# A four-layer stack on one core: which of every four scan steps hands its last product to GpSimd

## The chip, the cores and the metric

The kernel runs on one core of one Trainium2 chip. A core has five engines with a queue of instructions each: TensorE (PE, matmuls and transposes), VectorE (DVE), ScalarE (ACT), GpSimd (POOL) and SyncE (SP), which issues most of the transfers. An engine takes its instructions in order and waits at one whose operands are not ready. The metric is the time of one execution on the device in microseconds; the median over several runs counts.

## The reference, cut to what matters

Four layers follow each other over x of 4 x 512 x 256: a cross-attention block (L0), a self- and cross-attention block (L1), four selective-scan (Mamba) blocks (L2) and another attention block (L3). The change lies in L2. Each of its four blocks computes for every batch and each of 512 channels e, with 16 states s:

```
dt  = softplus(dt_low @ dtp_w + dtp_b)
dA  = exp(dt[..., None] * A)                        # decay of a state
dBu = dt[..., None] * Bm[:, :, None, :] * xi[..., None]
h   = da * h + dbu                                  # over time t
y_t = sum over s of h[e, s] * c[s]                  # the output map C
y   = (y + xi * D) * silu(z)
```

xi is a convolution of the block's input with a silu; Bm, Cm and dt_low are projections of xi.

## The kernel before, in words

Channels lie on the 128 partitions in four chunks (EC = 4), time on the free axis (T = 512). A **unit** is one block and one batch; there are 16 (NU), in order of block, then batch. A unit has two **pairs** of channel chunks, and a pair takes 16 **steps**: each step handles one chunk and two states, so one instruction covers 128 x 1024 values. Steps alternate between the two chunks of the pair; two steps share the loaded rows of B and C for their two states. A unit has 32 steps, all units together 512. In the text r is the step's number within its unit, from 0 to 31.

What a step i does:

- `maps` (L1625): SP loads the rows of B and C, spread over the partitions, as bB (3 buffers) and bC (4 buffers), four and five steps ahead.
- `product` (L1632): POOL computes dBu = dtx * bB, two steps ahead; dBu has four buffers. `begin` (L1649): ACT writes the start values into its first columns.
- `decay` (L1644): ACT computes two exponentials into ps_dA, a PSUM tile with two buffers, one step ahead.
- `states` (L1659): DVE runs the scan over time. 
- Then the states are multiplied by bC. For three steps of four DVE does it: the scan has written back into ps_dA, and `outputs_here` (L1666) multiplies ps_dA by bC into hC, four buffers. For the fourth, which `on_gpsimd` names, the scan writes to hP in SBUF (two buffers), and `outputs` (L1670) lets POOL multiply hP by bC in place, one step later.
- `add_up` (L1692): PE transposes and sums the products into ps_y: eight instructions of a 128 x 128 tile. DVE's products are added two steps after their scan, POOL's three steps after.

After 16 steps `close_pair` (L1708) lets DVE multiply ps_y by the gate zs into g, at the second step of the next pair. Beside the steps generators run that work out the next unit's input, advanced twice in each step: `front` (norm L1379 to L1421, ps_in by L185, xp L1443, convolution ps_cv by L178, xi L1430, xd L1468), `step` (ps_dt L1498, dt L1500, softplus L1309, dtx L1511, start values L1513 to L1519), `gate` (ps_z by L185, zs L1541), `gated` (ps_gt L1559, gT L1562, ps_out, hT_res L1574). The silus of xi and zs (`flush_silu`, L1723) come at r = 10 and 15. With the first batch of a block `front` also makes the block's diagonal weights on POOL (w_dg L1394, w_dD L1400).

The order on each queue is written out by hand, as one loop over the steps. Each pass issues, in this order: the silus, the loads, the exponentials of the next step, POOL's product two steps ahead, POOL's output of the step before, the closing of a pair, the scan, the transposes, and DVE's output, with the generators between.

Of the kernel before, what the change touches and what calls it, by code (L numbers as in the profile page):

```python
# [117 lines left out]

def on_gpsimd(i):

    return i % 4 == 1


@with_exitstack
def kernel(ctx: ExitStack, tc: tile.TileContext, t: dict, out: bass.AP):
# [1185 lines left out]
    def layer2(hT, A, far, h63, tail, X, fw, wl, late):  # L1311
# [5 lines left out]
        with ExitStack() as st:  # L1317
# [333 lines left out]
            def states(i):  # L1651
                if on_gpsimd(i):
                    hC = pool.tile([P, 2, T], F32, name="hP", tag="hP", bufs=2)
                else:
                    hC = pool.tile([P, 2, T], F32, name="hC", tag="hC", bufs=4)
                hCs[i] = hC
                dA = dAs[i].rearrange("p s t -> p (s t)")
                to = hC.rearrange("p s t -> p (s t)") if on_gpsimd(i) else dA
                nc.vector.tensor_tensor_scan(  # L1659
                    to, dA, dBus.pop(i).rearrange("p s t -> p (s t)"), 0.0, ALU.mult, ALU.add  # L1660
                )

            def outputs_here(i):
                dA = dAs.pop(i)
                if not on_gpsimd(i):
                    nc.vector.tensor_mul(hCs[i], dA, bmap[i // 2, 1])  # L1666
# [388 lines left out]
```

## Time and profile before

| | us |
|---|---|
| median of three runs | 4141.29 |
| lowest and highest | 4137.86, 4146.58 |
| profiled execution | 4144.32 |
| its span | 4142.5 |

| stretch of the span | us | PE busy | DVE busy | ACT busy | POOL busy |
|---|---|---|---|---|---|
| layers 0 and 1, to 1560 | 1560 | 1384 | 908 | 629 | 648 |
| before the first scan, to 1608 | 48 | 32 | 0.5 | 18 | 7 |
| scan block, unit 0, to 1720 | 112 | 94 | 93 | 73 | 97 |
| scan block, units 1 to 15, to 3430 | 1710 | 1373 | 1599 | 1106 | 1544 |
| layer 3 | 712.5 | 632 | 433 | 322 | 93 |

In the page, a group's line gives the line of code, engine, operation, output and inputs, the count, the busy time and the mean of one, and then the idle time of the engine just ahead of it with what ended that. In a timeline a row gives start, duration, engine, line and operands, and in brackets the idle time ahead of it and its releaser. A releaser is inferred: of several things waited for it is the one that came last by the profile.

### The profile page before, as it was taken

What the parts mean: (1) busy time and instruction counts of PE and PEld (TensorE: products, weight loads), DVE (VectorE), ACT (ScalarE), POOL (GpSimd) and SP (SyncE); (2) the same over time, 40 slices, a digit from 0 to 9 for tenths busy, and PEclk for the clock granted to TensorE, in tenths of its full rate; (3) what the DMA queues carried; (4) which work ended last, traced back from release to release, by engine and by line L of the source; (5) the groups of instructions that cost most, each with busy time, mean ns of one, the idle gap of its engine ahead of it and who ended that gap; (6) DMA issues with size and microseconds to landing.
All of it is one profiled execution on the core that took longest, in us unless ns stands there. A gap on an engine that the chain in (4) does not pass through costs nothing. (4 is left out here: it accounts for less than half of the span.)

```text
span 4142.5 us, 48645 instructions
## 1 busy us (share of the span) xinstructions
PE 3515.9 (85%) x17616; PEld 2204.8 (53%) x17616; DVE 3033.5 (73%) x2903; ACT 2148.3 (52%) x4366; POOL 2388.4 (58%) x1625
## 2 busy tenths in 40 slices
PE   7989998988898897888888788888887667999889
PEld 4654554545566464555555555555554444555446
DVE  5547567476555633999999999998999996676653
ACT  2345454454212424666666666666666553556422
POOL 2349269076100425899999999999998881000131
PEclk8999999999998998988988898888888778999999
DMA  2023022033100203444444444444443441000000
GB/s 75 11 85 103 25 82 92 17 96 94 44 1 0 66 22 104 152 150 154 153 159 148 150 157 159 158 153 149 158 154 138 143 155 36 1 1 1 1 6 16
DMA packets 140287, 369.93 MB, mean 89 GB/s; under 512 B 20624, under 2 KB 38224, under 8 KB 140048
## 3 DMA queue, kind: packets, MB, share of 16 engines
q1 hardware_dynamic: 136688, 363.58, 26.1%
q10 hardware_dynamic: 3360, 3.25, 0.3%
q8 instruction: 139, 2.28, 0.2%
q14 instruction: 100, 0.82, 0.1%
HBM read 363.50 MB, written 3.28 MB: 89 GB/s over the span
## 5 line engine op out<-in xcount | busy, mean ns | idle before, releaser
L1632 POOL TENSOR_TENSOR dBu<-dtx,bB 128x1022 f32<-128x1022 f32 x512 | 1199.0, 2362 | 65.9 <-DVE ps_dA L1659 65.9
L1659 DVE TENSOR_TENSOR_SCAN ps_dA<-ps_dA,dBu 128x1024 f32<-128x1024 f32 x384 | 878.3, 2287 | 131.6 <-POOL dBu L1632 91.8
L1644 ACT ACTIVATE ps_dA<-dt,A 128x512 f32<-128x512 f32 x1024 | 708.3, 692 | 428.5 <-DVE hC L1666 365.6
L1692 PE MATMUL ps_y<-ident,hC 128*128 128x128 f32 x3072 | 460.7, 302 | 104.1 <-DVE hC L1666 104.0
L1692 PEld LDWEIGHTS ps_y<-ident,hC 128*128 128x128 f32 x3072 | 403.9, 158 | 193.3 <-DVE hC L1666 122.4
L1666 DVE TENSOR_TENSOR hC<-ps_dA,bC 128x1024 f32<-128x1024 f32 x384 | 470.1, 1224 | 25.5 <-issue 0.4
L967 ACT ACTIVATE pr<-ps_s,nm 128x512 f32<-128x512 f32 x512 | 345.2, 686 | 260.2 <-DVE nm L963 260.2
L963 DVE TENSOR_REDUCE nm<-ps_s 128x2 f32<-128x1024 f32 x256 | 301.4, 1218 | 158.5 <-PE ps_s L952 144.2
L1670 POOL TENSOR_TENSOR hP<-hP,bC 128x1024 f32<-128x1024 f32 x128 | 302.1, 2360 | 89.2 <-issue 38.9
L981 PE MATMUL ps_pt<-ident,pr 128*128 128x128 f32 x2048 | 284.9, 279 | 66.9 <-DVE pT L986 33.2
L981 PEld LDWEIGHTS ps_pt<-ident,pr 128*128 128x128 f32 x2048 | 232.2, 142 | 165.0 <-issue 61.7
L1659 DVE TENSOR_TENSOR_SCAN hP<-ps_dA,dBu 128x1024 f32<-128x1024 f32 x128 | 291.8, 2280 | 2.9 <-ACT dBu L1649 2.2
L616 POOL TENSOR_TENSOR ln_rstd<-ln_rstd,const 128x4 f32<-128x4 f32 x24 | 24.4, 1018 | 443.8 <-DVE ln_rstd L615 442.2
L178 PE MATMUL ps_cv<-xp,w_dg 128*128 128x512 f32 x512 | 248.9, 619 | 30.9 <-ACT dBu L1649 25.3
L535 DVE TENSOR_TENSOR_SCAN phb<-pdA,phb 128x512 f32<-128x512 f32 x128 | 223.8, 1763 | 60.3 <-POOL phb L525 43.8
L984 ACT COPY pT<-ps_pt 128x512 f32<-128x512 f32 x256 | 140.6, 592 | 171.5 <-PE ps_pt L981 170.9
L1000 PE MATMUL ps_o<-pT,V 128*64 128x256 f32 (+1 forms) x2048 | 221.8, 393 | 1.8 <-ACT AT L1018 1.8
L952 PE MATMUL ps_s<-kT,qT 64*128 64x512 f32 (+1 forms) x1024 | 208.3, 644 | 2.2 <-DVE kT L1172 1.4
L525 POOL TENSOR_TENSOR phb<-hT_res,pm 128x512 f32<-128x512 f32 x128 | 188.4, 1476 | 34.0 <-DMA pm<-scrp 20.9
L1692 PE MATMUL ps_y<-ident,hP 128*128 128x128 f32 x1024 | 154.1, 300 | 54.6 <-POOL hP L1670 54.6
L784 POOL TENSOR_TENSOR pr<-pr,rs 128x512 f32<-128x512 f32 x64 | 65.4, 1043 | 225.2 <-DVE rs L782 219.3
L1692 PEld LDWEIGHTS ps_y<-ident,hP 128*128 128x128 f32 x1024 | 132.2, 155 | 109.6 <-POOL hP L1670 63.1
(276 smaller groups left out, 6399.2 us busy)
## 6 DMA issues: line engine op xcount, KB each, us to landing
bB<-scr SPq DMA_DIRECT2D x256, 512.0 KB, 4.1
bC<-scr SPq DMA_DIRECT2D x256, 512.0 KB, 3.8
pm<-scrp SPq DMA_DIRECT2D x224, 256.0 KB, 3.1
w_pw_in<-in_L_in SPq DMA_DIRECT2D x7, 512.0 KB, 4.5
X<-in_x SPq DMA_DIRECT2D x4, 512.0 KB, 7.2
w_L_W<-in_L_W SPq DMA_DIRECT2D x2, 1024.0 KB, 10.4
w_L_Wq<-in_L_Wq SPq DMA_DIRECT2D x2, 1024.0 KB, 6.4
w_L_Wo<-in_L_Wo SPq DMA_DIRECT2D x2, 1024.0 KB, 9.0
```

Source lines behind the costliest of these rows:

```text
L178: nc.tensor.matmul(dst, l, r, start=(i == 0), stop=(i == len(pairs) - 1))
L535: nc.vector.tensor_tensor_scan(hb, dA, hb, 0.0, ALU.mult, ALU.add)
L963: nc.vector.tensor_reduce(nm, ps, AX.X, ALU.max, negate=True)
L967: nc.scalar.activation(pr, ps[:, x, :], AF.Exp, bias=nm[:, x : x + 1], accum_out=rs[:, y : y + 1])
L981: nc.tensor.transpose(pp[:, t4, :], pr[:, t4 * P : (t4 + 1) * P], ident)
L1000: nc.tensor.matmul(ps_o[0][j * stride : (j + 1) * stride, half * W2 : (half + 1) * W2], Vs[n][0][:, t4, h * stride : (h + 1) * stride], pT ...
L1632: nc.gpsimd.tensor_mul(dBu[:, :, 1:], dtx[:, 1:].unsqueeze(1).broadcast_to([P, 2, T - 1]), bmap[i // 2, 0][:, :, 1:])
L1644: nc.scalar.activation(dA, dt, AF.Exp, scale=A[:, l, m, s : s + 1])
L1659: nc.vector.tensor_tensor_scan(to, dA, dBus.pop(i).rearrange("p s t -> p (s t)"), 0.0, ALU.mult, ALU.add)
L1666: nc.vector.tensor_mul(hCs[i], dA, bmap[i // 2, 1])
L1670: nc.gpsimd.tensor_mul(hCs[i], hCs[i], bmap[i // 2, 1])
L1692: nc.tensor.matmul(y[:, j, k * P : (k + 1) * P], hC[:, s, j * P : (j + 1) * P], ident, is_transpose=True, start=False, stop=(2 * s2 + s == ...
```

## The change

POOL multiplies the first step of every four (r = 0, 4, 8, ...) instead of the second (r = 1, 5, 9, ...). The number of products on each engine stays the same. With it move: the scans that write hP, the places of POOL's and DVE's products in their queues, and the transposes of both in PE's queue, since POOL's step is added three steps after its scan and DVE's two.

```
 def on_gpsimd(i):
-    return i % 4 == 1
+    return i % 4 == 0
```

What reads it:

```
def states(i):
    if on_gpsimd(i):
        hC = pool.tile([P, 2, T], F32, name="hP", tag="hP", bufs=2)
    else:
        hC = pool.tile([P, 2, T], F32, name="hC", tag="hC", bufs=4)
...
for j in (i - 3, i - 2):
    if 0 <= j < NU * US and on_gpsimd(j) == (j == i - 3):
        add_up(j)
```

## The prediction

> **What bounds the kernel now.** The views were read from the whole to one step. First the page's busy shares and its 40 slices: they say which engine is full where. In the scan block (1608 to 3430 us; slices 16 to 33) VectorE (DVE) stands at 9 tenths nearly throughout, TensorE and GpSimd (POOL) at 8 to 9.
>
> ```profile
> span 4142.5 us, 48645 instructions
> PE 3515.9 (85%) x17616; PEld 2204.8 (53%) x17616; DVE 3033.5 (73%) x2903; ACT 2148.3 (52%) x4366; POOL 2388.4 (58%) x1625
> DVE  5547567476555633999999999998999996676653
> POOL 2349269076100425899999999999998881000131
> L1659 DVE TENSOR_TENSOR_SCAN ps_dA<-ps_dA,dBu 128x1024 f32<-128x1024 f32 x384 | 878.3, 2287 | 131.6 <-POOL dBu L1632 91.8
> L1666 DVE TENSOR_TENSOR hC<-ps_dA,bC 128x1024 f32<-128x1024 f32 x384 | 470.1, 1224 | 25.5 <-issue 0.4
> L1670 POOL TENSOR_TENSOR hP<-hP,bC 128x1024 f32<-128x1024 f32 x128 | 302.1, 2360 | 89.2 <-issue 38.9
> ```
>
> The change adds and removes no instruction: 384 products stay on DVE, 128 on POOL. So only DVE's idle time between steps can move. I went through DVE's timeline, numbered the scans (512 steps, 16 units of 32, r is the step within its unit) and listed every wait over 0.3 us. They recur at fixed places: before r=11 in all 16 units (4.39 us in unit 0, 3.16 in units 1 to 14, 1.74 in unit 15), before r=3 (2.24 in unit 0, 0.56 in twelve others), before r=19 (0.90 to 1.27 in units 1 to 14), and 4.10 before g in units 3, 7 and 11. The page blames POOL for most of them, so I looked at one, in ScalarE's (ACT) timeline and then DVE's (unit 11, r=8 to 11):
>
> ```profile
> 2888.36 1.42 ACT L1644 ACTIVATE ps_dA<-dt,A 128x512 f32<-128x512 f32 x2 [0.94 <-DVE hC L1666]
> 2889.71 0.18 ACT L1649 COPY dBu<-h 128x2 f32<-128x2 f32 x1
> 2889.89 1.28 ACT L1723 ACT_TABLE_LOAD   x1
> 2891.19 1.92 ACT L1723 ACTIVATE xi<-xi 128x2048 f32<-128x2048 f32 x1
> 2893.01 1.89 ACT L1723 ACTIVATE zs<-zs 128x2048 f32<-128x2048 f32 x1
> 2894.92 1.28 ACT L1644 ACT_TABLE_LOAD   x1
> 2896.21 1.42 ACT L1644 ACTIVATE ps_dA<-dt,A 128x512 f32<-128x512 f32 x2
> ...
> 2884.78 2.29 DVE L1659 TENSOR_TENSOR_SCAN ps_dA<-ps_dA,dBu 128x1024 f32<-128x1024 f32 x1
> 2887.10 1.22 DVE L1666 TENSOR_TENSOR hC<-ps_dA,bC 128x1024 f32<-128x1024 f32 x1
> 2888.24 2.28 DVE L1659 TENSOR_TENSOR_SCAN hP<-ps_dA,dBu 128x1024 f32<-128x1024 f32 x1
> 2890.44 0.67 DVE L1574 TENSOR_TENSOR hT_res<-ps_out,hT_res 128x512 f32<-128x512 f32 x1
> 2891.02 2.29 DVE L1659 TENSOR_TENSOR_SCAN ps_dA<-ps_dA,dBu 128x1024 f32<-128x1024 f32 x1
> 2893.34 1.22 DVE L1666 TENSOR_TENSOR hC<-ps_dA,bC 128x1024 f32<-128x1024 f32 x1
> 2897.73 2.30 DVE L1659 TENSOR_TENSOR_SCAN ps_dA<-ps_dA,dBu 128x1024 f32<-128x1024 f32 x1 [3.17 <-POOL dBu L1632]
> ```
>
> The last exponential of step 11 ends at 2896.21 + 1.42 = 2897.63, the scan starts at 2897.73. The dBu it reads had been made about 9.9 us before (POOL's products counted the same way); POOL merely ended a later one at that moment. So ACT ends this wait: two silus and two table loads stand between the exponentials of steps 10 and 11. At r=3 and r=19 it is the softplus with its two loads.
>
> **The rule that follows.** ps_dA has two buffers, so the exponentials of step r can start when step r-2 has let its buffer go: after its scan if POOL multiplies, after its product if DVE does. From there DVE runs steps r-1 and r before it wants step r+1. A step with its product takes 2.32 + 1.14 = 3.46 us from start to start (2891.02 to 2893.34, 2887.10 to 2888.24), one without 2.20 (2888.24 to 2890.44). Work behind the exponentials of step r therefore has 6.92 us of cover if DVE multiplies both r-1 and r, and 5.66 if POOL takes one of them: 1.26 less. POOL's step is now 1 modulo 4, so the short covers are at r = 1 and 2 modulo 4. After the change they are at 0 and 1: r = 2, 6, 10, 18 gain 1.26, r = 0, 8, 24 lose 1.26, the others keep theirs. The instruction order of the built programs agrees: ACT's and SP's queues are unchanged line for line, only PE, DVE and POOL move.
>
> **Part by part.**
> - r=11, silus behind step 10: 16 waits of at least 1.74, each shorter by 1.26: **-20.2**. At least 0.9 each if ACT isn't free when scan 8 ends.
> - r=3, softplus behind step 2: twelve waits of 0.56 go (-6.7), unit 0's loses 1.26: **-8.0**.
> - r=19, softplus behind step 18: eleven waits (units 1, 3 to 5, 7 to 9, 11 to 14), 10.2 in all, go: **-10.2**. In units 2, 6 and 10 nothing: POOL has four w_dg products and w_dD there, and its next hP product now comes ahead of rstd instead of behind it (2.36 later, less the 1.15 that POOL idled ahead of this burst), so rstd, ps_rb and DVE's hn come 1.2 later, which takes the 0.90.
> - r=25, xi waiting for ps_cv behind step 24: the cover shrinks. The slack between the last exponential and the scan is now 0.1 in units 0, 1 and 11, 0.8 to 1.0 in 5, 8, 9 and 12, about 2 or more elsewhere; 0.1 is the hand-over. Loss: 3 x 1.26 + (0.56 + 0.36 + 0.36 + 0.46) = **+5.5**.
> - r=9, zs waiting for ps_z behind step 8: slack 0.9 in all units, so 0.46 x 16 = 7.4 would be lost. But on PE the fourth ps_z group now stands ahead of step 4's eight transposes instead of behind them, and one group is 0.87 from start to start: taken at **0**, upper end +7.4.
> - r=1, 5, 13, 17, 21, 29: slack 1.2 to 2.6 (most 1.9 or 2.0) against 1.26: 0.
> - g in units 3, 7, 11 waits for PE, which runs without a gap for 20 us ahead of it. After hn, PE has one transpose group less ahead of its convolutions: 3 x 0.87 = **-2.6**; ends 0 and -2.7.
> - POOL: the same work. Past unit 0 its products are ready 4.5 us or more before their scans (2.5 at the start of units 3, 7, 11), but 0.3 to 3.0 in units 2, 6 and 10 from r=22 on: 0 to 3 x 2.36 = +7.1, taken at 0, since hP moves behind product 23 instead of 24 and the burst is 1.1 ahead of that.
> - bC: read first by POOL and last by DVE a step sooner, so its buffer comes free earlier; SP loses nothing. hT_res and hn adds that now fall between a scan and its product hide the 0.13 us that scan-to-product takes over 2.20: up to -4, left out. The last steps (r=29 to 31 of unit 15) end on DVE either way: 0.
>
> Sum: -20.2 - 8.0 - 10.2 + 5.5 - 2.6 = -35.5 us. The profiled execution took 4144.3 (span 4142.5 and 1.8 around it), which gives 4108.8; it stood 3.0 over the median of 4141.3, which I take for scatter, so against the median 4105.8.
>
> **The clock, as a rival on the other side.** TensorE's granted clock is not steady in a unit: 0.50 from 2228 to 2252 us (PE busy, but with gaps of 1.6 to 2.7 us ahead of it), then 0.99, and again slow at ps_in after DVE's hn: its four rows take 3.65 us instead of 1.95. Slow stretches there set r=25. ps_cv took 6.50 us at the slow clock in unit 0 and 3.67 otherwise, and in the changed order it follows ps_in directly, with no transposes between. If PE stays slow over ps_cv (+2.83), the next ps_in (+1.77) and two transpose groups (+1.74), a unit loses 6.3; in the ten units with this work (1, 3 to 5, 7 to 9, 11 to 13) that is 63, and 4141.3 - 35.5 + 63 = 4169. It decides from 3.6 us a unit on. Against it: in those ten units before, the slow clock ended within some 6 us of ps_in's start.
>
> [...]
>
> **Other rivals.** ACT isn't free at the early release: zs behind ps_z holds step 9's exponentials. Then r=11 gains 0.9 instead of 1.26 (16 x 0.36 = 5.8 lost) and r=9 costs 7.4: 4119. It speaks for it that ACT waited 2.91 us for that ps_z. Or POOL's bursts, ACT and PE together eat the gain: no change, 4141; POOL's slack of 0.3 us in three units speaks for it, its 4.5 us elsewhere against. Or a little more is gained: the waits at r=30 (0.35 to 1.01 in five units, 3.0 in all) and the 4 us of scan-to-product gaps go too: 4099.
>
> **How the numbers follow.** A difference under 0.2% (8 us) can't be told from none. Forecast 4106, with an own range of 4092 to 4116 that holds the 4099: 0.60. ACT late, 4119: 0.18. No change, 4133 to 4149: 0.11. Slower by the clock, 4169: 0.11. Faster 0.78, same 0.11, slower 0.11. The range leaves out the slower case and part of no change: 4090 to 4138.
>
> **What would show it.** Right: ACT's order unchanged, DVE's wait before r=11 at 1.9 us and before r=3 and r=19 gone in most units, ACT's wait on the scan of hP before step 10 instead of on hC; small new waits at r=25. Wrong: waits at r=9 or r=25 of over 1 us in most units, ps_cv at 6.5 us after hn, or DVE's waits in units 2, 6 and 10 grown past what they were.

## The result, and the profile after

| | before | after |
|---|---|---|
| median of four runs, us | 4139.57 | 4094.32 |
| lowest and highest | 4137.60, 4146.58 | 4090.23, 4095.76 |
| profiled execution | 4144.32 | 4095.76 |
| its span | 4142.5 | 4093.9 |
| first scan to last g | 1607.62 to 3432.65 | 1607.02 to 3383.96 |

The ratio is 0.9882, 95% interval 0.987 to 0.9894: 45 us less by the medians, 48.6 by the two profiled executions. From the first scan to the last g the block went from 1825.0 to 1776.9 us, 48.1 less; what lies before it and behind it kept its time to within 1 us.

The page of the kernel after: the span, DVE's row of the 40 slices, and the groups of DVE's scans and products (at the end of a group, the idle time just ahead of it and what ended most of that).

```profile
span 4093.9 us, 48583 instructions
DVE  5538567466465643899999999999999996676653
L1659 DVE TENSOR_TENSOR_SCAN ps_dA<-ps_dA,dBu 128x1024 f32<-128x1024 f32 x384 | 877.1, 2284 | 37.1 <-ACT ps_dA L1644 28.9
L1666 DVE TENSOR_TENSOR hC<-ps_dA,bC 128x1024 f32<-128x1024 f32 x384 | 469.7, 1223 | 24.4
L1659 DVE TENSOR_TENSOR_SCAN hP<-ps_dA,dBu 128x1024 f32<-128x1024 f32 x128 | 291.8, 2280 | 53.9 <-POOL dBu L1632 49.2
```

The work is the same: 384 scans of 2.28 us, 384 products of 1.22. Only the idle time moved. The 131.6 us ahead of the scans into ps_dA became 37.1; the 49.2 now shown ahead of the scans into hP is the wait before the very first scan, which stood in the other group before, since step 0 has changed its form. That start is nearly the same in both (47.5 us before, 49.2 after). Without it, 84.1 us ahead of the scans into ps_dA became 37.1.

To leave the start and the end of the block out, here are DVE's waits from 1720 to 3300 us, first of the kernel before, then after (total, times, longest).

```profile
DVE ps_dA L1659 <- POOL dBu L1632: 44.3, 14, 3.2
DVE ps_dA L1659 <- ACT ps_dA L1644: 19.4, 27, 1.1
DVE g L1708 <- PE ps_y L1692: 12.3, 3, 4.1
```

```profile
DVE ps_dA L1659 <- ACT ps_dA L1644: 21.6, 12, 2.0
DVE g L1708 <- PE ps_y L1692: 7.1, 3, 2.5
DVE ps_dA L1659 <- ACT dBu L1649: 4.5, 4, 2.0
DVE hT_res L1574 <- PE ps_out L178: 4.3, 7, 0.8
DVE hn L1421 <- PE ps_rb L1414: 2.4, 3, 0.9
```

The 14 waits of 3.2 us that the page had put down to POOL are waits of 2.0 us and less, now put down to ACT, as they should have been. They are shorter, not gone; small new ones stand before hT_res and hn.

The same place in unit 11 as in the prediction, r = 8 to 11, ACT's timeline and then DVE's, of the kernel after:

```profile
2850.18 1.42 ACT L1644 ACTIVATE ps_dA<-dt,A 128x512 f32<-128x512 f32 x2 [0.67 <-DVE hP L1659]
2851.54 0.18 ACT L1649 COPY dBu<-h 128x2 f32<-128x2 f32 x1
2851.72 1.28 ACT L1723 ACT_TABLE_LOAD   x1
2853.01 1.91 ACT L1723 ACTIVATE xi<-xi 128x2048 f32<-128x2048 f32 x1
2854.83 1.90 ACT L1723 ACTIVATE zs<-zs 128x2048 f32<-128x2048 f32 x1
2856.74 1.28 ACT L1644 ACT_TABLE_LOAD   x1
2858.04 1.42 ACT L1644 ACTIVATE ps_dA<-dt,A 128x512 f32<-128x512 f32 x2
...
2847.87 2.28 DVE L1659 TENSOR_TENSOR_SCAN hP<-ps_dA,dBu 128x1024 f32<-128x1024 f32 x1
2850.07 2.27 DVE L1659 TENSOR_TENSOR_SCAN ps_dA<-ps_dA,dBu 128x1024 f32<-128x1024 f32 x1
2852.28 0.69 DVE L1574 TENSOR_TENSOR hT_res<-ps_out,hT_res 128x512 f32<-128x512 f32 x1
2852.88 1.21 DVE L1666 TENSOR_TENSOR hC<-ps_dA,bC 128x1024 f32<-128x1024 f32 x1
2854.01 2.29 DVE L1659 TENSOR_TENSOR_SCAN ps_dA<-ps_dA,dBu 128x1024 f32<-128x1024 f32 x1
2856.34 1.22 DVE L1666 TENSOR_TENSOR hC<-ps_dA,bC 128x1024 f32<-128x1024 f32 x1
2859.56 2.30 DVE L1659 TENSOR_TENSOR_SCAN ps_dA<-ps_dA,dBu 128x1024 f32<-128x1024 f32 x1 [2.00 <-ACT ps_dA L1644]
```

ACT does the same 7.86 us from the start of step 10's exponentials to the start of step 11's (2850.18 to 2858.04; before, 2888.36 to 2896.21). What differs is when that stretch begins as seen from DVE. The exponentials of step 10 now start when scan 8 ends (2850.15), with DVE's scan 9 only beginning; before, they started when product 8 ended (2888.32). DVE has one product more to do while ACT is away, and the wait falls from 3.17 to 2.00.

By places, from the two DVE timelines (waits over 0.3 us, all units, in us):

| place | before | after | change | forecast |
|---|---|---|---|---|
| r=11 | 50.4 | 28.3 | -22.1 | -20.2 |
| hT_res at r=7 and r=9, ahead of it | 0 | 4.3 | +4.3 | 0 |
| r=3 | 8.96 | 2.23 | -6.7 | -8.0 |
| r=19 | 13.2 | 0.4 | -12.8 | -10.2 together |
| hn at r=23, units 2, 6, 10 | 0 | 2.4 | +2.4 | with the line above |
| r=25 | 2.9 | 3.2 | +0.3 | +5.5 |
| r=9 | 0 | 0 | 0 | 0 |
| g in units 3, 7, 11 | 12.3 | 7.1 | -5.2 | -2.6 |
| last g | 1.2 | 2.1 | +0.9 | 0 |
| r=30 | 3.0 | 0.9 | -2.1 | 0 |
| unit 0, r=7, 10, 24 | 7.1 | 5.2 | -1.9 | 0 |
| everything else, as what is left | | | -5.2 | left out |
| first scan to last g | 1825.0 | 1776.9 | -48.1 | -35.5 |

### The profile page after: what moved, and what is told of

The parts are those of the page before. It is cut to its first block, busy times and chain, and to the rows that moved or that the text cites. A ratio compares the mean times of both kernels' runs of the same rounds, so it can differ in the third digit from the quotient of the medians.

```text
span 4093.9 us, 48583 instructions
## 1 busy us (share of the span) xinstructions
PE 3488.9 (85%) x17616; PEld 2194.8 (54%) x17616; DVE 3034.5 (74%) x2903; ACT 2148.5 (52%) x4366; POOL 2384.8 (58%) x1625
## 3 DMA queue, kind: packets, MB, share of 16 engines
q8 instruction: 139, 2.28, 0.2%
HBM read 363.50 MB, written 3.28 MB: 90 GB/s over the span
## 5 line engine op out<-in xcount | busy, mean ns | idle before, releaser
L1632 POOL TENSOR_TENSOR dBu<-dtx,bB 128x1022 f32<-128x1022 f32 x512 | 1199.9, 2364 | 47.6 <-DVE ps_dA L1659 47.5
L1659 DVE TENSOR_TENSOR_SCAN ps_dA<-ps_dA,dBu 128x1024 f32<-128x1024 f32 x384 | 877.1, 2284 | 37.1 <-ACT ps_dA L1644 28.9
L1692 PE MATMUL ps_y<-ident,hC 128*128 128x128 f32 x3072 | 443.3, 295 | 89.9 <-DVE hC L1666 89.9
L1692 PEld LDWEIGHTS ps_y<-ident,hC 128*128 128x128 f32 x3072 | 388.3, 153 | 175.0 <-DVE hC L1666 120.3
L1659 DVE TENSOR_TENSOR_SCAN hP<-ps_dA,dBu 128x1024 f32<-128x1024 f32 x128 | 291.8, 2280 | 53.9 <-POOL dBu L1632 49.2
L1692 PE MATMUL ps_y<-ident,hP 128*128 128x128 f32 x1024 | 167.0, 317 | 66.5 <-POOL hP L1670 66.5
L1692 PEld LDWEIGHTS ps_y<-ident,hP 128*128 128x128 f32 x1024 | 145.8, 167 | 113.7 <-POOL hP L1670 72.3
```

The costliest lines, as they stand in the source:

```text
L1632: nc.gpsimd.tensor_mul(dBu[:, :, 1:], dtx[:, 1:].unsqueeze(1).broadcast_to([P, 2, T - 1]), bmap[i // 2, 0][:, :, 1:])
L1659: nc.vector.tensor_tensor_scan(to, dA, dBus.pop(i).rearrange("p s t -> p (s t)"), 0.0, ALU.mult, ALU.add)
L1692: nc.tensor.matmul(y[:, j, k * P : (k + 1) * P], hC[:, s, j * P : (j + 1) * P], ident, is_transpose=True, start=False, stop=(2 * s2 + s == ...
```

## The experiments

**The theory** is the rule of the prediction: ACT's work behind the exponentials of step r has as cover what DVE does in steps r-1 and r, which is 1.26 us less when POOL multiplies one of the two. The rivals: that it only matters to move POOL's product away from some place, whatever the new one; that the order on TensorE made the gain; that the waits come from the silus and the softplus in some other way than through the cover.

**Fourteen small copies at one step.** If the rule holds, the same piece of ACT work must cost more behind step 14 than behind step 16 in the kernel before (POOL has r = 13 and 17, so 14 is short), and less in the kernel after (POOL has r = 12 and 16, so 16 is short). Added to both kernels, with `r == 16` in two of the four:

```
+            idle = pool.tile([P, P], F32, name="idle", tag="idle", bufs=1)
+            nc.gpsimd.memset(idle, 0.0)
...
+                    if main and r == 14:
+                        for _ in range(14):
+                            nc.scalar.copy(idle, ident)
```

> The kernel before, plus 14 copies of a 128x128 tile on ScalarE behind the exponentials of step 14 of each unit (result unused; some 4 us in all, estimated from 0.58 us for a 128x512 copy and 0.18 for a 128x2 one). Theory (cover of steps r-1 and r): steps 13 and 14 contain GpSimd's step 13, so 0.7 us of idle ScalarE and 1.9 of slack, 2.6 in all, stand against 4.0: 1.4 x 16 units = +22 us, as DVE waits before r=15. Rival (the gain comes from TensorE's order or clock, or from GpSimd's queue, not from this cover): the place of the copies makes no difference, the same cost at step 14 and at step 16.

> The kernel before, plus the same 14 copies behind the exponentials of step 16. Theory: steps 15 and 16 are both DVE's, 2.0 us idle and 1.9 of slack, 3.9 against 4.0: +0 to +5 us, some 20 less than at step 14. Rival: the same as at step 14.

> The changed kernel, plus the same 14 copies behind step 14. Theory: steps 13 and 14 are both DVE's now, cover 3.9: +0 to +5 us over the changed kernel (ratio to before 0.988 to 0.990). Rival: the same as at step 16.

> The changed kernel, plus the same 14 copies behind step 16. Theory: step 16 is GpSimd's now, cover 2.6: +22 us over the changed kernel (ratio to before about 0.994), the mirror image of the two runs on the kernel before. Rival: the same as at step 14.

| copies behind | step 14 | step 16 |
|---|---|---|
| kernel before (alone 4143.13) | 4176.09, ratio 1.0077 (1.0062 to 1.0092) | 4159.81, ratio 1.0040 (1.0025 to 1.0054) |
| kernel after (alone 0.9882 of before) | 4106.39, ratio 0.9909 (0.9895 to 0.9924) | 4132.41, ratio 0.9974 (0.9964 to 0.9983) |

The copies took 4.58 us together. Here is DVE's first wait behind them in unit 5, one line from each of the four timelines, in the order before 14, before 16, after 14, after 16.

```profile
2245.66 2.30 DVE L1659 TENSOR_TENSOR_SCAN ps_dA<-ps_dA,dBu 128x1024 f32<-128x1024 f32 x1 [1.77 <-ACT ps_dA L1644]
```

```profile
2244.18 2.29 DVE L1659 TENSOR_TENSOR_SCAN hP<-ps_dA,dBu 128x1024 f32<-128x1024 f32 x1 [0.41 <-ACT ps_dA L1644]
```

```profile
2216.46 2.30 DVE L1659 TENSOR_TENSOR_SCAN ps_dA<-ps_dA,dBu 128x1024 f32<-128x1024 f32 x1 [0.45 <-ACT ps_dA L1644]
```

```profile
2235.08 2.30 DVE L1659 TENSOR_TENSOR_SCAN ps_dA<-ps_dA,dBu 128x1024 f32<-128x1024 f32 x1 [1.72 <-ACT ps_dA L1644]
```

The picture is the mirror image that the rule asks for: 1.77 and 0.41 before, 0.45 and 1.72 after. The short cover costs 1.36, 1.32, 1.27 and 1.31 us more than the long one, whichever two neighbours are compared, against 1.26 by the rule. The absolute sizes were all set too low. Against the same kernel without copies, the cost was 33 us (step 14) and 17 us (step 16) in the kernel before, where 22 and 0 to 5 had been expected, and 11 and 38 us in the kernel after, where 0 to 5 and 22 had been expected. The copies were 4.58 us long and not 4.0, so the long covers did not hide them. Behind step 16 a further cost shows in 13 units: in the kernel before, rstd waits 0.93 us for ps_r, and in the kernel after r = 19 waits another 0.54. There the copies also hold up ACT's evictions of ps_dt; in unit 5 of the kernel before TensorE sits idle for 4.24 us ahead of ps_r until the first of them ends.

**POOL at the third step of four.** The kernel before with `return i % 4 == 2`. All the products move, and the orders on TensorE, DVE and POOL change as much as they do in the change studied.

> GpSimd multiplies the third step of every four (2 modulo 4). Theory: the short covers are then at r = 2 and 3 modulo 4, so the silus behind step 10 and the softplus behind steps 2 and 18 keep the short cover they had before: waits before r=3, 11 and 19 as before (0.6, 3.2, 0.9 us), ratio to before 0.998 to 1.004. Rival (moving GpSimd's step away from the closing of a pair, or TensorE's order, brings the gain): faster than before by 20 us or more.

Measured: 4135.92 against 4142.73, ratio 0.9990 (0.9981 to 1.0000). The rule puts the short covers at r = 2 and 3 modulo 4 here, so steps 2, 10 and 18, which carry the softplus and the silus, are as short as before. The waits agree: 3.28 before r = 11 (3.16 before), 1.00 before r = 19 (0.90), 0.46 before r = 3 (0.56). Moving the product is by itself worth 8 us at most here (0.9981 is the lower end) of the 45 that the change brought; what counts is which steps lose their cover.

**The work moved instead of the product.** The kernel before with the silus one step later, so that they have the long cover:

```
-                    if main and r in (10, 15):
+                    if main and r in (11, 15):
```

> The kernel before, with the first silus one step later (r = 11 instead of 10), GpSimd's step left at the second. Theory: behind step 11 the cover is long (steps 10 and 11 are DVE's), so the wait of 3.2 us before r=11 becomes one of about 1.9 before r=12: 16 x 1.26 = -20 us, ratio 0.995, with no transposes or products moved between engines' queues. Rival (the gain belongs to the moved products and transposes): no change.

The edit moves both silus of a unit: in the trace of the kernel before, xi's and zs's run together at the first of the two places in 14 of the 16 units, and the call at r = 15 finds work only once.

Measured: 4154.70 against 4142.73, ratio 1.0027 (1.0017 to 1.0036). This expectation failed: the kernel is slower, not faster. The term it was about came out: 1.83 us before r = 12 in units 1 to 14 where 3.16 had stood before r = 11. But before r = 20 there are now 3.15 us in units 1 to 13, where r = 19 had cost 0.90. Unit 1, ACT's timeline and then TensorE's:

```profile
1786.69 1.42 ACT L1644 ACTIVATE ps_dA<-dt,A 128x512 f32<-128x512 f32 x2 [0.67 <-DVE hP L1659]
1789.03 0.69 ACT L1500 ACTIVATE dt<-ps_dt,cols 128x512 f32<-128x512 f32 x1 [0.92 <-PE ps_dt L1498]
1791.88 0.69 ACT L1500 ACTIVATE dt<-ps_dt,cols 128x512 f32<-128x512 f32 x1 [2.16 <-PE ps_dt L1498]
...
1783.42 3.57 PE L185 MATMUL ps_r<-const,hn 128*128 128x1 f32 x16 [0.46 <-ACT hn L1379]
1786.93 2.07 PE L1498 MATMUL ps_dt<-xd,w_dt 16*128 16x512 f32 x2
1789.77 2.07 PE L1498 MATMUL ps_dt<-xd,w_dt 16*128 16x512 f32 x2 [0.78 <-ACT dt L1500]
```

A unit's front waits for its silu, so the whole chain xi, ps_x, xd, ps_dt is one step later. The front of the unit after next still begins at r = 16, and its 16 matmuls for the mean square (ps_r, 3.57 us) now stand ahead of ps_dt in TensorE's queue, where they stood behind it. ACT waits 0.92 and 2.16 us for ps_dt, and the exponentials of step 20 stand behind that. The profiled execution of this kernel was 4143.92, 11 us under its median; what made the others longer, no trace shows.

**The same, with the order restored.** If that is the cause, starting the front one step later too must take the wait before r = 20 away:

```
-            FS = 16
+            FS = 17
...
-                    if main and r in (10, 15):
+                    if main and r in (11, 15):
```

> The kernel before with the silus behind step 11, as in the run before this one that missed, and now the front of the unit after next begun one step later too (at step 17 in place of 16). In the run that missed, the silus cost 1.83 us before step 12 where they had cost 3.16 before step 11, as the cover says, but every unit showed 3.15 us before step 20, where 0.88 before step 19 had been: ScalarE's evictions of ps_dt waited 0.92 and 2.16 us for TensorE, which had the 16 matmuls of ps_r for the front ahead of them, 3.57 us. Theory: the front one step later puts ps_r behind ps_dt again, and the softplus stands behind step 19, whose cover is the long one: before step 20 0 to 0.4 us; 14 x (1.33 + 0.5 to 0.9) = -26 to -31 us, ratio 0.992 to 0.996. Rival (the loss came from xi's chain one step later as such, through xd, the copy to DRAM or the gathering of dt): 2 to 3.2 us stay before step 20, ratio 1.000 to 1.004.

Measured: 4111.92 against 4140.61, ratio 0.9932 (0.9917 to 0.9946), inside the theory's numbers. TensorE's timeline of unit 1 has the old order again:

```profile
1787.16 3.78 PE L1498 MATMUL ps_dt<-xd,w_dt 16*128 16x512 f32 x4
1793.20 3.58 PE L185 MATMUL ps_r<-const,hn 128*128 128x1 f32 x16 [2.27 <-ACT dt L1500]
```

No unit waits over 0.3 us before r = 19 or 20, and 1.83 stands before r = 12. So 29 us come from shifting ACT's two pieces of work by one step while POOL keeps its place: the rule works from both sides. What this kernel does not have is the gain at r = 3 (0.56 is still there), and it pays new waits before r = 4 in units 3, 7 and 11 (2.35, 1.26 and 1.26) and before g in units 1 and 14 (4.32 and 3.61).

**The two silus apart.** The remaining 2.00 us before r = 11 should go if zs's silu (1.9 us) is taken out of that stretch. xi's stays behind step 10, zs's goes behind step 15, at the price of two more table loads. In the kernel after:

```
-                while to_silu:
+                while any(r is xi for r in to_silu):
                     yield
...
-            def flush_silu():
-                for r in to_silu:
-                    r = r.rearrange("p a b -> p (a b)")
+            def flush_silu(n=2):
+                for _ in range(min(n, len(to_silu))):
+                    r = to_silu.pop(0).rearrange("p a b -> p (a b)")
                     nc.scalar.activation(r, r, AF.Silu)
-                to_silu.clear()
...
-                        flush_silu()
+                        flush_silu(1 if r == 10 else 2)
```

> The changed kernel, with only the silu of xi at r = 10 and that of zs at r = 15 (with two more table loads). Theory: the wait before r=11 (1.2 to 2.0 us) shrinks by the 1.9 us of zs's silu to 0.1 or 0.2; the new work behind step 15 (1.28 + 1.89 + 1.28 = 4.5 us) has a cover of 3.9 and costs 0.5 us: 14 x (1.8 - 0.5) = -18 us against the changed kernel, ratio to before 0.984. If the wait before r=11 was not ScalarE's: no gain, and the loads cost 7 us.

Measured: 4079.59 against 4142.73, ratio 0.9853 (0.9838 to 0.9868), the best of all kernels here. Unit 1, DVE's scans of r = 11 and r = 16:

```profile
1760.00 2.30 DVE L1659 TENSOR_TENSOR_SCAN ps_dA<-ps_dA,dBu 128x1024 f32<-128x1024 f32 x1 [0.20 <-ACT dBu L1649]
...
1776.94 2.29 DVE L1659 TENSOR_TENSOR_SCAN hP<-ps_dA,dBu 128x1024 f32<-128x1024 f32 x1 [0.56 <-ACT ps_dA L1644]
```

The 2.00 are gone (0.20 is left) and 0.56 has come before r = 16. The two profiled executions lie 18.5 us apart, the ratios 0.0029, which is 12 us (4 to 20 with the intervals of both taken together): the gain was forecast at 18.

The same edit in the kernel before:

> The kernel before with xi's silu alone behind step 10 and zs's behind step 15. The cover of step 10 is the short one here (GpSimd has step 9), that of step 15 the long one. With the kernel after, xi's silu alone behind step 10 left a wait of 0.20 us before step 11 and zs's behind step 15 one of 0.56 us before step 16. Theory (cover): before step 11 0.20 + 1.26 = 1.46 us in place of 3.16, before step 16 0.56 us as there; 14 x (1.70 - 0.56) = -16 us, ratio 0.994 to 0.998. Rival (the splitting is worth the same whichever step GpSimd has): 3.16 to about 1.2 or less by the 2.0 us that it took away after, or to 0.2, and no wait before step 16; ratio 0.991 to 0.993. The rest of the unit's waits (3: 0.56, 19: 0.88) stay.

Measured: 4127.16 against 4140.61, ratio 0.9967 (0.9955 to 0.9980). Unit 8, the same two scans:

```profile
2546.55 2.30 DVE L1659 TENSOR_TENSOR_SCAN ps_dA<-ps_dA,dBu 128x1024 f32<-128x1024 f32 x1 [1.37 <-ACT ps_dA L1644]
...
2563.50 2.30 DVE L1659 TENSOR_TENSOR_SCAN ps_dA<-ps_dA,dBu 128x1024 f32<-128x1024 f32 x1 [0.57 <-ACT dBu L1649]
```

With one silu alone behind step 10, the two kernels differ by 1.37 - 0.20 = 1.17 us there, and not at all behind step 15, whose cover is long in both. The forecast by the cover (1.46 and 0.56 us, 0.994 to 0.998) came out, and the numbers written down for the rival (1.2 us or less, no wait before step 16, 0.993 at most) did not. The rival itself, that splitting is worth the same in either kernel, is not refuted by this: the split takes 1.80 us from the wait before r = 11 in both kernels (3.17 to 1.37, 2.00 to 0.20) and puts 0.56 or 0.57 before r = 16 in both. The cover asks for that too, as long as the shortened work still outlasts it. So this run gives the two covers once more, 1.17 us apart, but doesn't separate the two accounts. That POOL's step decides where work is cheap rests on the copies and on the moved silus.

**rstd first on POOL.** The kernel after has new waits of 0.54 to 0.91 us before hn in units 2, 6 and 10, because rstd's power stands behind the diagonal weights on POOL. Here it comes ahead of them:

```
                 rstd = pool.tile([P, TPB], F32, name="rstd", tag="rstd")
                 nc.vector.tensor_scalar(rstd, ps[:, :TPB], EPS, None, ALU.add)
                 done(ps)
+                yield
+                nc.gpsimd.tensor_tensor(rstd, rstd, mhalf, ALU.pow)
                 if b == 0:
...
-                yield
-                nc.gpsimd.tensor_tensor(rstd, rstd, mhalf, ALU.pow)
                 yield
                 yield
```

> The changed kernel, with rstd taken on GpSimd ahead of the diagonal weights instead of behind them (units 2, 6 and 10; in the other units the same place but one advance earlier). Theory: the waits of hn for ps_rb in these units (0.5 to 0.9 us) go, TensorE isn't held ahead of ps_rb and its backlog ends sooner, so the waits before g in units 3, 7 and 11 (2.2 to 2.5 us) shrink to under 1: -5 to -9 us against the changed kernel, ratio to before 0.986 to 0.988. Rival (hn and g are late because of the transposes' new order): no change.

Measured: 4098.68 against 4142.73, ratio 0.9898 (0.9884 to 0.9913): no gain, the expectation failed. The waits before hn are gone, but in their place, in unit 2, at r = 24 and 25:

```profile
1919.48 2.29 DVE L1659 TENSOR_TENSOR_SCAN hP<-ps_dA,dBu 128x1024 f32<-128x1024 f32 x1 [0.82 <-POOL dBu L1632]
1922.45 2.30 DVE L1659 TENSOR_TENSOR_SCAN ps_dA<-ps_dA,dBu 128x1024 f32<-128x1024 f32 x1 [0.68 <-POOL dBu L1632]
```

They add up to 4.1 us in the three units against the 2.4 taken away. The other half of the expectation failed as well: the waits before g in units 3, 7 and 11 are 2.4 us, where under 1 had been expected. At r = 24 and 25 POOL is what DVE waits for: its product for step 24 ends at 1919.45, that for step 25 at 1922.42, each 0.03 us ahead of its scan. In the kernel after, these two products of unit 2 had 1.2 and 0.4 us to spare. Now DVE comes to step 24 0.9 us sooner, and POOL's product comes 1.0 later, counted from scan 23. POOL is later because it sits idle for 0.55 us ahead of dtx (ended by the softplus) and 0.36 ahead of rstd, a stretch that the first diagonal weight had filled. Another order that keeps POOL busy there was not tried.

## Why the prediction was right, and where its sizes were off

The forecast was 4105.8, with 4092 to 4116 as the likeliest case's own range; the median is 4094.32. Step by step:

- **The bound and the misread releaser.** Right. The page blamed POOL for the waits before r = 11; after the change it blames ACT for the same place, with POOL's dBu product ready earlier than the scan in both. The four kernels with copies show that ACT's lateness alone makes such waits.
- **The rule of the cover.** Right, from both sides: 1.27 to 1.36 us in the copies against 1.26, 1.33 where the silus were moved (3.16 to 1.83), 1.17 where one silu was left.
- **r=11, -20.2.** -22.1: units 1 to 14 gave 1.16 where nothing else happens (3.16 to 2.00) and up to 1.92 where an hT_res wait of up to 0.69 came just ahead and took its part; those waits (4.3 in all) were not in the sum. The 0.10 missing from 1.26 stands in the two timelines of unit 11: with hT_res's add in it, step 9 takes 3.94 us from scan to scan with its product (2850.07 to 2854.01) and 2.78 without (2888.24 to 2891.02), a difference of 1.16. The prediction saw that such an add hides 0.13 us between scan and product, but not that this shortens the cover of step 10. Unit 0 gave 0.88, unit 15 all its 1.74.
- **r=3 and r=19.** Right: the twelve waits at r=3 are gone, but unit 0's stayed at 2.23, as there ACT is behind on its own work and the release isn't what it waits for. r=19 went in all units but unit 6 (0.36), and hn's wait of up to 0.91 in units 2, 6, 10 is the loss that was put there: together -10.4 against -10.2.
- **r=25, +5.5.** The step that failed: +0.3. Only unit 0's wait grew (2.24 to 3.21); two of 0.3 in units 1 and 11 went, and the small new waits that had been named as a sign did not come. The sum took its slacks from the kernel before and assumed that they would carry over. The low ones, 0.1 to 1.1, were those of units 1, 5, 8, 9, 11 and 12, in which TensorE ran slow at ps_in (four matmuls in 2.81 to 3.75 us, granted clock 0.50 to 0.67); units 3, 4, 7 and 13, in which it ran at full speed there (1.95 or 1.96 us, clock 1.00), had 1.9 or 2.0. After the change the slack is 0.66 in all ten, which is about what the rule makes of 2.0 (2.0 - 1.26 = 0.7). The slow stretch itself had gone: ps_in's clock in both kernels is the subject of the last section.
- **g, -2.6.** -5.2, outside the ends given. The transposes were counted rightly: ahead of the g of unit 3 TensorE has ten groups of eight from ps_in's start on, where it had eleven (0.87 us each). The sum left out the clock. Counted from the first hn, DVE comes to that g after 32.56 us in both kernels, but TensorE ends its last transposes after 34.77 us instead of 36.62. The first ps_in takes 1.72 us from start to start instead of 3.48 (granted clock 1.00 in units 2, 6 and 10, where it had been 0.50 to 0.53), and a gap of 0.77 ahead of a ps_cv is gone; against that ps_in starts 1.5 later after hn. In the three units 1.59 to 1.86 of wait went.
- **Gaps and r=30.** The rival "a little more is gained" had them in part. r=30 gave 2.1 of 3.0. Everything else gave about 5 where "up to 4" had been left out, but only some 2 of it lies in and between scans and products; 2.6 are thirteen waits of 0.2 us ahead of rstd for ps_r, which are gone and which nobody had listed.
- **The clock, 4169.** Did not come: in units 1 to 13 ps_cv's eight matmuls after hn took 3.67 to 3.84 us of TensorE, at a granted clock of 1.00. Only unit 0 had them slow, 6.16 us at 0.59, as before (6.50 at 0.56).
- **ACT late, 4119.** Did not come: no wait stands before r=9 (slack 0.7 in most units, 0.2 at least), and r=11 gained more than 0.9.

The 12.6 us between the sum and the block are, in that order of size: r=25 (5.2), everything else (5.2), r=30 (2.1), r=11 and unit 0 (1.9 each), g and the last g together (1.7), less the hT_res waits (4.3) and r=3 (1.3). The mechanism and its three large terms (r=11, r=3, r=19) were right; that the total stayed inside the range, near its lower end, is in part luck, since misses of 18 us on one side met 5.6 on the other.

## What to carry to other kernels

Where one engine fills a double buffer for another and does side work between fills, the time it may be away is what the consumer does between the release of one buffer and its need of the next; a step with less work on the consumer, or one that lets the buffer go earlier, moves that time by its own length (1.26 us in the timeline before the change, 1.16 to 1.36 in the waits measured here). Put the side work behind the steps with the longest cover, or, as here, put the short steps elsewhere, and before shifting either, look at what else starts at a fixed step, since a chain that comes one step later can fall behind something that it used to precede. Read a wait's releaser against the operands: an operand made 9.9 us ago, as POOL's dBu here, isn't what was waited for.

## What the runs showed of the hardware that was not expected

TensorE ran slow at the first ps_in in nine of units 1 to 13 of the kernel before and in none of them in the kernel after. Here are ps_in's four matmuls in unit 1, of the kernel before and then of the kernel after; the granted clock over them was 0.50 and 1.00.

```profile
1809.17 3.75 PE L185 MATMUL ps_in<-hn,w_inx 128*128 128x512 f32 x4 [2.82 <-ACT ps_dA L1644]
```

```profile
1802.26 1.96 PE L185 MATMUL ps_in<-hn,w_inx 128*128 128x512 f32 x4 [0.87 <-DVE hn L1421]
```

In units 1 to 13 of the kernel before, the gap ahead of the first ps_in was 2.1 to 2.9 us, and in nine of the thirteen the four matmuls took 2.81 to 3.75 us, at a granted clock of 0.50 to 0.67; in the other four 1.95 or 1.96, at 1.00. In the kernel after, ten of these units show gaps of 0.87 to 1.62 us, and the group took 1.95 or 1.96 in all ten; in units 2, 6 and 10 it follows transposes without a gap and took 1.88. The granted clock was 1.00 in all thirteen. The gap is shorter because DVE has less to do ahead of hn. TensorE's last work before the gap is the transposes of step 19. Then hn follows scan 21, and the product of step 20 in between is now POOL's. In unit 13 hn starts 5.57 us after product 19 ends in the kernel before, and 4.29 in the kernel after. With the shorter gaps TensorE's clock was 1.00 at ps_in, and with that the r=25 loss of the prediction fell away.

The length of the gap alone does not decide: in the kernel before, after 2.90 us, ps_in was at full speed in three units (3, 7 and 13) and slow in one (9). Here is the slow case, unit 9, and one of the three fast ones, unit 13, each with the stretch of the gap and that of the four matmuls (length, busy time and count of PE, PEld, DVE, ACT and POOL, then the granted clock, DMA share, GB/s).

```profile
2708.51 2.81 PE L185 MATMUL ps_in<-hn,w_inx 128*128 128x512 f32 x4 [2.90 <-ACT ps_dA L1644]
2705.61:2708.51 2.90, 0.01 (x1) 0.03 (x1) 2.90 (x3) 2.84 (x7) 2.90 (x4) 1.00 0.45 175
2708.51:2711.32 2.81, 2.81 (x5) 1.18 (x6) 2.78 (x3) 0.67 (x1) 2.81 (x2) 0.67 0.03 13
...
3158.41 1.95 PE L185 MATMUL ps_in<-hn,w_inx 128*128 128x512 f32 x4 [2.90 <-ACT ps_dA L1644]
3155.51:3158.41 2.90, 0.00 (x2) 0.03 (x1) 2.90 (x3) 2.84 (x7) 2.90 (x4) 1.00 0.55 178
3158.41:3160.36 1.95, 1.95 (x6) 0.94 (x7) 1.95 (x2) 0.66 (x1) 1.95 (x2) 1.00 0.03 13
```

The granted clock was 1.00 through the gap in both, and over the matmuls behind it 0.67 in unit 9 and 1.00 in unit 13. What sets the two apart was not tested. That the shorter gap is what kept the clock in the kernel after is therefore the author's estimate, from thirteen units of each kernel: 9 of 13 slow behind 2.1 to 2.9 us, none of 13 behind 1.62 us or less (10 units) or no gap (3).
